# A two-layer decoder on one core: pass B of the first self attention in nine sets, statistics by chunk, and mixes in halves

## The chip, the cores and the metric

The kernel runs on one core of a Trainium2 chip. The metric is the device time of one launch in microseconds (us), and lower is better. The core has a matrix engine (TensorE, in the profile PE, with its weight loads as PEld), a vector engine (VectorE, DVE), a scalar engine (ScalarE, ACT), a general engine (GpSimd, POOL) and a synchronisation engine (SyncE, SP), which here only issues transfers. Each engine runs its own list of instructions in order; they wait for each other by semaphores.

## The reference, cut to what matters

The input x is (batch 4, sequence 1024, width 256), the context (4, 154, 256). Two decoder layers follow each other; every sublayer is added to its input and normalised.

```python
def _layernorm(x, axis=-1, eps=1e-05):
    m = mean(x); v = var(x)
    return (x - m) / sqrt(v + eps)

# layer 0: self attention, 16 heads of 16, causal
scores = einsum('bhqd,bhkd->bhqk', q * scale, k) + causal_bias
out = softmax(scores) @ v;  out = out @ w_out.T + b_out
x = layernorm(x + out)
# layer 0: cross attention, 16 heads of 64, over the 154 context rows
# layer 0: feed forward with rounded activations and weights and a convolution
# layer 1: self attention, one head of 256, softmax over axis 1
# layer 1: cross attention, 16 heads of 16, keys and values from the context, padding mask
# layer 1: feed forward
x_prev = concatenate([zeros, x[:, :-1]], axis=1)
xr = mu_r * x + (1 - mu_r) * x_prev
xk = mu_k * x + (1 - mu_k) * x_prev
out = sigmoid(xr @ W_r) * (square(relu(xk @ W_k)) @ W_v)
x = layernorm(x + out)
```

## The kernel before

All of x stays in on-chip memory for the whole launch: one tile per batch, eight chunks of 128 rows, 256 wide. Each stage function makes a list of events, `at(when, function, arguments)`, and `run_in_order` calls them by their number `when`. Every TensorE instruction and some others are marked to keep that order on their engine; the rest is placed by the framework's planner, which orders the instructions of VectorE, ScalarE and GpSimd itself. `layernorm` takes the statistics of its chunks at once (L136 and L137), asks GpSimd for the inverse root (L141), and leaves the normalising instructions (`last_step`: L156 on VectorE, or L147 and L152 on ScalarE) on a list of pending work; `run_in_order` counts six events down and then runs it, and `settle` runs all that is pending for a batch, which a function that reads x calls first.

**First self attention** (function `self_attention`, profile lines L178 to L480). Sixteen head sets of four heads follow each other, four per batch; T = 20 units of event time are one head set. For head set s two passes run at once. Pass A computes the scores with queries as rows, only to find each query's maximum (`a_unit`, L319 and L335 on VectorE). Then `shifted_queries` turns the maxima (nmt, L344 on VectorE, transposes L351 on TensorE) and adds them to the padded queries (L355), so that in pass B the scores come out less their maximum. Pass B (`b_unit`) computes the scores of head set s - 1 with keys as rows, ScalarE takes the exponential (L385), GpSimd clears the upper triangle (L388), and `weighted` multiplies by the values into an accumulator (tiles acc). Keys come in chunks of 128, queries in halves of 512; the causal triangle makes some pieces narrower: a set is what shares a bank of 512. Pass B has ten sets, the sets 2 and 9 being 256 wide, and pass A has nine units; each is done as two pairs of heads, and `together` interleaves one pair of A with one pair of B, so that the four row groups of the array hold four 32-row matmuls at once. Eighteen such pairs fill the units 1 to 18; the tenth set of B has a place of its own at 19. Then comes the boundary: the weighting of set 7 at 18.5, the tenth set at 19, the weighting of set 8 at 20.1, the shifted queries at 20.3, the weighting of set 9 at 20.4.

Seven banks of the accumulation memory hold the score tiles and everything else that TensorE makes in this stage; a new tile waits until the one seven before it was read.

Beside this stand fillers: projections of keys, queries and values, transposes, and for a finished batch the output: `normalised`, `turned_back`, and `out_projected` (tile s from wo and onT, then y = s + bias at L474 and two additions to x at L479 and L480, whose maximum and minimum with 0 leave out what is not a number). The output runs in four places per batch at 11.5 and 15.5 of two head sets, two chunks a place, with a layernorm of four chunks after every second. For the last batch they stand one after another at the end, before cross attention, whose first step is to transpose x (L652, copy xT at L655).

**Last stage** (`cross_attention_and_feed_forward`, L1215 on). Cross attention of layer 1 goes head set by head set; the exponentials are L1349, the weighted sum is acc, `normalised` is L1380 to L1384, `turned` L1396, `out_projected` L1412. For a batch that is through with it, `shifted_x` transposes x into fx with a zero column ahead (L1433, copies L1436), `mix` makes the two mixes m1 and m0 (L1442 on ScalarE, then L1443 on VectorE) from 1024 columns at a time, `squared` (L1453, L1454) and `fed_forward` (L1466 to L1469) finish, and the result is normalised on ScalarE and stored. The last batch has the same schedule as the others and nothing beside it.

The other three stages (cross attention of layer 0, feed forward and self attention of layer 1) use the same `layernorm`, after the last of four chunks was added.

## Time and profile before

| what | value |
|---|---|
| time, median of 3 runs | 2303.15 us (2297.65 to 2305.23) |
| the profiled execution | 2305.49 us |
| its span | 2303.8 us |
| first self attention | about 31 to 780 us |
| cross attention, first feed forward | about 780 to 1430 |
| self attention of layer 1, rest of the feed forward | to about 1845 |
| cross attention of layer 1, feed forward | about 1845 to 2304 |

The profile is one execution. A line of a timeline has the start in us from the span's beginning, the duration, the engine, the line of the kernel, the operation, the tiles (written <- read) with their shapes, and the count of instructions that it merges; in square brackets it says how long the engine had been idle before it and what ended that. The row PEclk of the page shows in forty slices what clock TensorE was granted, in tenths of full speed.

### The profile page before, as it was taken

How to read it: one execution, taken by the hardware profiler on the slowest of the kernel's cores; microseconds unless marked ns; L12 is line 12 of the kernel's file. 1: busy time of each engine (PE TensorE's matmuls, PEld its weight loads, DVE VectorE, ACT ScalarE, POOL GpSimd, SP SyncE). 2: the span in 40 equal slices, each digit the busy share in tenths (PEclk: the TensorE clock that was granted, in tenths of full speed). 3: DMA queues.
4: the chain of work that ended last, by engine and by line, in shares of the span. 5: the costliest groups of instructions: out<-in, count | busy, mean ns of one | idle time of the engine just before them, and what ended most of it. 6: DMA issues, size and time to landing. Idle time of an engine off the chain costs nothing.

```text
span 2303.8 us, 38032 instructions
## 1 busy us (share of the span) xinstructions
PE 2172.9 (94%) x14228; PEld 1275.8 (55%) x14228; DVE 1482.0 (64%) x3223; ACT 1127.3 (49%) x2909; POOL 507.7 (22%) x1113
## 2 busy tenths in 40 slices
PE   7999999999999999999999998879989999999996
PEld 4444444454444556656556556556666755565645
DVE  4666666666666555558997887775873365555644
ACT  1455554554455465456656664444442234434354
POOL 1111111111112265444454432000000021111101
PEclk9999999999999999999999999989999999999998
DMA  3201100000000100000000000000000010010101
GB/s 89 55 7 33 39 23 15 10 15 15 6 15 1 38 1 19 1 1 1 1 1 1 33 1 21 1 1 1 1 1 1 2 20 15 10 32 11 28 1 37
DMA packets 24440, 34.78 MB, mean 15 GB/s; under 512 B 5952, under 2 KB 19648, under 8 KB 24256
## 3 DMA queue, kind: packets, MB, share of 16 engines
q1 hardware_dynamic: 22640, 31.20, 5.8%
q8 instruction: 113, 1.85, 0.3%
q10 hardware_dynamic: 1616, 1.16, 0.2%
q14 instruction: 71, 0.58, 0.1%
HBM read 15.56 MB, written 4.19 MB: 9 GB/s over the span
## 4 chain that ended last, share of the span: by engine, by line
PE 73%; DVE 19%; ACT 5%; issue 1%; POOL 1%; DMA 1%; SPq 0%; ACTq 0%; DVEq 0%; POOLq 0%
PE s L178 22%; PE t L568 15%; PE s L1166 10%; PE s L568 9%; PE acc L178 6%; DVE gt L917 4%; PE acc L1166 3%; PE t L752 2%; ACT u L727 2%; DVE bnst L136 1%; DVE x L156 1%; DVE nmp L319 1%; DVE nmx L723 1%; PE t L1075 1%; DVE ht L903 1%
## 5 line engine op out<-in xcount | busy, mean ns | idle before, releaser
L385 ACT ACTIVATE p<-s 128x512 f32<-128x512 f32 (+1 forms) x640 | 319.5, 554 | 296.3 <-PE s L178 293.6
L319 DVE TENSOR_REDUCE nmp<-s 128x1 f32<-128x512 f32 (+3 forms) x640 | 298.9, 524 | 156.4 <-PE s L178 156.4
L178 PE MATMUL s<-qs,kp 32*128 32x512 f32 (+3 forms) x1536 | 370.1, 531 | 2.7 <-DVE nmp L319 2.7
L178 PE MATMUL s<-kp,qp 32*128 32x128 f32 (+3 forms) x2304 | 330.2, 408 | 5.6 <-DVE nmp L319 3.5
L735 POOL TENSOR_SCALAR p<-u,rs 128x128 f32<-128x128 f32 x512 | 214.5, 437 | 290.5 <-DVE rs L731 196.1
L178 PEld LDWEIGHTS s<-kp,qp 32*128 32x128 f32 x2304 | 168.0, 188 | 142.9 <-issue 43.1
L388 POOL TENSOR_SCALAR_AFFINE_SELECT p<-p 128x256 f32<-128x256 f32 x256 | 100.6, 408 | 650.1 <-ACT p L385 650.1
L727 ACT ACTIVATE u<-s,nmx 128x154 f32<-128x154 f32 x512 | 192.0, 388 | 31.6 <-DVE nmx L723 27.1
L178 PEld LDWEIGHTS s<-qs,kp 32*128 32x128 f32 x1536 | 143.9, 186 | 65.0 <-DVE nmp L319 28.0
L141 POOL TENSOR_TENSOR rstd<-ve,neghalf 128x4 f32<-128x4 f32 (+1 forms) x56 | 55.3, 987 | 539.2 <-DVE ve L139 502.1
L178 PE MATMUL acc<-p,v 128*32 128x512 f32 (+3 forms) x1536 | 164.4, 508 | 1.1 <-ACT ot L427 0.8
L568 PEld LDWEIGHTS s<-kt,qt 64*128 64x128 f32 x1024 | 102.5, 188 | 71.6 <-issue 53.6
L568 PE MATMUL s<-kt,qt 64*128 64x154 f32 x1024 | 136.5, 316 | 0.5 <-ACT qt L709 0.3
L723 DVE TENSOR_REDUCE nmx<-s 128x4 f32<-128x616 f32 x128 | 101.2, 790 | 50.2 <-PE s L568 50.2
L568 PE MATMUL t<-xT,xw 128*128 128x512 f32 x256 | 122.4, 601 | 7.5 <-DVE xT L655 4.4
L1323 DVE TENSOR_REDUCE nmt<-s 128x3 f32<-128x462 f32 (+1 forms) x192 | 99.0, 579 | 46.4 <-PE s L1166 46.4
L917 DVE SCALAR_TENSOR_TENSOR gt<-ht,cw,gt 128x256 f32<-128x256 f32 x256 | 117.9, 501 | 6.6 <-ACT gt L913 5.5
L568 PE MATMUL t<-v,pt 128*128 128x256 f32 x512 | 117.7, 383 | 3.3 <-DVE pt L1076 2.9
L568 PE MATMUL s<-qt,xT 128*128 128x512 f32 x256 | 120.0, 613 | 0.0
L568 PE MATMUL t<-xw,ot 128*128 128x256 f32 x512 | 116.3, 381 | 3.6 <-ACT pr L756 1.9
L335 DVE TENSOR_REDUCE nmp<-s 128x4 f32<-128x512 f32 x128 | 82.6, 688 | 49.9 <-PE s L178 49.9
L568 PEld LDWEIGHTS t<-v,pt 128*128 128x128 f32 x512 | 97.1, 192 | 24.3 <-issue 6.2
(257 smaller groups left out, 3886.5 us busy)
## 6 DMA issues: line engine op xcount, KB each, us to landing
qp<-sq SPq DMA_DIRECT2D x128, 64.0 KB, 2.3
kp<-sk SPq DMA_DIRECT2D x64, 64.0 KB, 2.3
out_dram<-x SPq DMA_DIRECT2D x8, 512.0 KB, 2.9
x<-in_x_dram SPq DMA_DIRECT2D x3, 1024.0 KB, 5.4
wf<-in_L_ffn_w_dram SPq DMA_DIRECT2D x2, 1024.0 KB, 5.9
xw<-in_L_xattn_wk_dram SPq DMA_DIRECT2D x1, 1024.0 KB, 5.0
xw<-in_L_xattn_wq_dram SPq DMA_DIRECT2D x1, 1024.0 KB, 5.1
xw<-in_L_xattn_wv_dram SPq DMA_DIRECT2D x1, 1024.0 KB, 5.0
```

Of the source, the lines that this page charges most:

```text
L178: pe(nc.tensor.matmul(o, l, r, start=start, stop=stop))
L319: nc.vector.tensor_reduce(nmp[:, 2 * pair + g, qc, i : i + 1], t[g][:, c0 : c0 + n], AX.X, ALU.max)
L335: nc.vector.tensor_reduce(nmp[:, 2 * pair + g, q0 : q0 + 4, 0], t[g].rearrange("p (j n) -> p j n", j=4), AX.X, ALU.max,)
L385: nc.scalar.activation(p[:, g, :total], t[g][:, :total], AF.Exp)
L388: nc.gpsimd.affine_select(out=v, in_=v, compare_op=ALU.is_ge, fill=0.0, base=0, pattern=[[0, 2], [1, P]], channel_multiplier=-1,)
L568: pe(nc.tensor.matmul(o, l, r, start=start, stop=stop))
L723: nc.vector.tensor_reduce(nmx.rearrange("p i g -> p g i"), t, AX.X, ALU.max, negate=True)
L727: nc.scalar.activation(u[:, 2 * i + g, :], t[:, g, i, :], AF.Exp, bias=nmx[:, i, g : g + 1], accum_out=ssum[:, i, g : g + 1],)
L735: nc.gpsimd.tensor_scalar(p[:, h * P : (h + 1) * P], u[:, h, :P], rs[:, h : h + 1], 1.0, ALU.mult, ALU.mult)
L917: nc.vector.scalar_tensor_tensor(g, ht[:, i, k : k + N], cw[:, hc, k : k + 1], g, ALU.mult, ALU.add)
L1166: pe(nc.tensor.matmul(o, l, r, start=start, stop=stop))
L1323: nc.vector.tensor_reduce(nmts[s % 2][:, 3 * u : 3 * u + n, g, 17], ts[g][:, : n * LK].rearrange("p (c k) -> p c k", k=LK), AX.X, ALU.max, ...
```

## The change

Pass B: the sets are now lists of (half, key chunk, place in the bank). The 256 columns of key chunk 6 go into set 2 beside the 256 of key chunk 2, so there are nine sets of 512 and no place at 19. The weighting of chunk 6 has an event of its own at 10.6, and the weighting of set 8 is the last of the head set, at 20.4, behind the shifted queries. Output: eight places with one chunk each, y in a tile of its own, and after each chunk its statistics are taken (`measured`), so `layernorm` of four chunks finds them made; the same in cross attention, in self attention of layer 1 and in both places of the last stage. Mixes: by halves of 512 columns; for batches 0 to 2 `shifted_x` stands at the same event times as before (u is 16 earlier), the mix m1 at 18.4 to 25.6 and m0 at 30.4 to 42.4. For the last batch the whole chain from the turning to the feed forward runs by halves of the sequence, and `settle` can be asked for a half. The last layernorm of all waits one event instead of six.

```diff
...
-    def settle(b=None):
-
-        for p in [p for p in pending if b in (None, p[1])]:
+    def settle(b=None, c0=None):
+
+        for p in [p for p in pending if b in (None, p[1]) and c0 in (None, p[3])]:
             pending.remove(p)
...
-    def layernorm(b, c0, n, scalar=False, then=None):
+    measures = {}
+
+    def measured(b, c):
+
+        if c % 4 == 0:
+            measures[b, c // 4] = small.tile([P, 4, nc.vector.BN_AGGR_DIM], F32, tag="bnmv", name="bnmv", bufs=6)
+        st = small.tile([P, nc.vector.BN_STATS_DIM], F32, tag="bnst", name="bnst", bufs=2)
+        nc.vector.bn_stats(st, xs[b][:, c, :])
+        nc.vector.bn_aggr(measures[b, c // 4][:, c % 4, :], st)
+
+    def layernorm(b, c0, n, scalar=False, then=None, wait=6):
...
         xb = xs[b][:, c0 : c0 + n, :]
-        st = small.tile([P, 4, nc.vector.BN_STATS_DIM], F32, tag="bnst", name="bnst", bufs=2)
-        mv = small.tile([P, 4, nc.vector.BN_AGGR_DIM], F32, tag="bnmv", name="bnmv", bufs=3)
-        for c in range(n):
-            nc.vector.bn_stats(st[:, c, :], xb[:, c, :])
-            nc.vector.bn_aggr(mv[:, c, :], st[:, c, :])
+        if n == 4:
+            mv = measures.pop((b, c0 // 4))
+        else:
+            st = small.tile([P, 2, nc.vector.BN_STATS_DIM], F32, tag="bnst2", name="bnst2", bufs=2)
+            mv = small.tile([P, 2, nc.vector.BN_AGGR_DIM], F32, tag="bnmv2", name="bnmv2", bufs=3)
+            for c in range(n):
+                nc.vector.bn_stats(st[:, c, :], xb[:, c, :])
+                nc.vector.bn_aggr(mv[:, c, :], st[:, c, :])
         ve = small.tile([P, 4], F32, tag="ve", name="ve", bufs=2)
...
         rstd = small.tile([P, 4], F32, tag="rstd", name="rstd", bufs=3)
...
-        pending.append([6, b, last_step])
+        pending.append([wait, b, last_step, c0])
...
-        b_sets = [(0, [(0, 0)]), (0, [(1, 0), (3, 384)]), (0, [(2, 0)])]
-        b_sets += [(1, [(k, 0)]) for k in range(4)]
-        b_sets += [(1, [(4, 0)]), (1, [(5, 0), (7, 384)]), (1, [(6, 0)])]
+        b_sets = [[(0, 0, 0)], [(0, 1, 0), (0, 3, 384)], [(0, 2, 0), (1, 6, 256)]]
+        b_sets += [[(1, k, 0)] for k in range(5)]
+        b_sets += [[(1, 5, 0), (1, 7, 384)]]
...
         def b_unit(s, i, pair):
-            qh, pieces = b_sets[i]
+            pieces = b_sets[i]
             t = [bank() for _ in range(2)]
...
             rows = [slice(64 * pair + 32 * g, 64 * pair + 32 * g + 32) for g in range(2)]
-            total = sum(width(qh, kc) for kc, _ in pieces)
             rounds = []
-            for kc, c0 in pieces:
+            for qh, kc, c0 in pieces:
                 n = width(qh, kc)
...
                     (
...
                 for g in range(2):
-                    nc.scalar.activation(p[:, g, :total], t[g][:, :total], AF.Exp)
-                for c0 in [c0 for kc, c0 in pieces if kc >= 4 * qh]:
+                    nc.scalar.activation(p[:, g, :], t[g], AF.Exp)
+                for c0 in [c0 for qh, kc, c0 in pieces if kc >= 4 * qh]:
                     v = p[:, :, c0 : c0 + P]
...
                         out=v, in_=v, compare_op=ALU.is_ge, fill=0.0, base=0,
...
-        def weighted(s, i):
+        def weighted(s, qh, i, pieces, first=False, last=False):
             b, t4 = divmod(s, 4)
-            qh, pieces = b_sets[i]
-            first, last = i in (0, 3), i in (2, 9)
             if first:
...
             acc = accs[s, qh]
-            p2 = [pts.pop((s, i, pair)) for pair in range(2)]
+            p2 = [pts[s, i, pair] for pair in range(2)]
             for kc, c0 in pieces:
...
                 for g in range(4):
...
                         first,
-                        last,
+                        last and kc == pieces[-1][0],
                     )
...
                 if qh == 0:
...
-        def out_projected(b, i):
+        def out_projected(b, c):
             onT = ots[b, "n"]
-            t = bank()
-            for j in range(2):
-                c = 2 * i + j
-                for e in range(2):
-                    mm(
-                        t[:, j * E : (j + 1) * E],
-                        onT[:, e, c * P : (c + 1) * P],
-                        l0a_wo[:, e, :],
-                        e == 0,
-                        e == 1,
-                    )
-            y = wk.tile([P, 2, 512], F32, tag="p", name="y0", bufs=6)[:, :, :E]
-            nc.vector.tensor_tensor(
-                y, t.rearrange("p (c n) -> p c n", c=2), bo2.unsqueeze(1).to_broadcast([P, 2, E]), ALU.add
-            )
-
-            xb = xs[b][:, 2 * i : 2 * i + 2, :]
+            t = bank()[:, :E]
+            for e in range(2):
+                mm(t, onT[:, e, c * P : (c + 1) * P], l0a_wo[:, e, :], e == 0, e == 1)
+            y = wk.tile([P, E], F32, tag="y0", name="y0")
+            nc.vector.tensor_tensor(y, t, bo2, ALU.add)
+
+            xb = xs[b][:, c, :]
             nc.vector.scalar_tensor_tensor(xb, y, 0.0, xb, ALU.max, ALU.add)
             nc.vector.scalar_tensor_tensor(xb, y, 0.0, xb, ALU.min, ALU.add)
-            if i % 2:
-                layernorm(b, 2 * i - 2, 4)
+            measured(b, c)
+            if c % 4 == 3:
+                layernorm(b, c - 3, 4)
...
                 at(t0 + 5 * T + 3.5 + 4 * i, turned_back, b, e, q)
-                at(t0 + (i // 2 + 7) * T + (11.5, 15.5)[i % 2] if b < 3 else t0 + 6 * T + i, out_projected, b, i)
+            for c in range(NC):
+                u = (117.5, 135.5, 151.5, 155.5, 157.5, 171.5, 175.5, 177.5)[c]
+                at(t0 + u if b < 3 else t0 + 6 * T + c, out_projected, b, c)
         for i in range(2 * NB):
...
             for q in range(2):
...
                 at((s + 2) * T + 1.5 + 4 * i, normalised, s, i)
-            for i in range(10):
-                at((s + 1) * T + (2 * i + 4.5 if i < 8 else 20.1 + 0.3 * (i - 8)), weighted, s, i)
+            t0 = (s + 1) * T
+            at(t0 + 4.5, weighted, s, 0, 0, [(0, 0)], True)
+            at(t0 + 6.5, weighted, s, 0, 1, [(1, 0), (3, 384)])
+            at(t0 + 8.5, weighted, s, 0, 2, [(2, 0)], False, True)
+            for k in range(5):
+                at(t0 + 10.5 + 2 * k, weighted, s, 1, 3 + k, [(k, 0)], k == 0)
+            at(t0 + 10.6, weighted, s, 1, 2, [(6, 256)])
+            at(t0 + 20.4, weighted, s, 1, 8, [(5, 0), (7, 384)], False, True)
         for i, (w, name) in enumerate(((l0x_wk, "k"), (l0x_wq, "q"), (l0x_wv, "v"))):
...
         for s in range(4 * NB + 1):
...
                 at(s * T + 1 + j, together, *units)
-            if s > 0:
-                at(s * T + 19, together, *[(b_unit, s - 1, 9, pair) for pair in range(2)])
         run_in_order(events)
...
             nc.vector.tensor_tensor(xs[b][:, c, :], t[:, :E], xs[b][:, c, :], ALU.add)
+            measured(b, c)
             if k == 3:
...
             )
+            measured(b, c)
             if c % 4 == 3:
...
             nc.vector.tensor_tensor(xb, t.rearrange("p (c n) -> p c n", c=2), xb, ALU.add)
+            for c in range(2 * i, 2 * i + 2):
+                measured(b, c)
             if i % 2:
...
         def shifted_x(b, e, q):
-            settle(b)
+            settle(b, 4 * q)
             t = bank()
...
                 pe(nc.tensor.transpose(
...
-        def mix(b, i, e):
-            if e == 0:
+        def mix(b, i, e, q):
+            if (e, q) == (0, 0):
                 mixed[b, i] = wk.tile([P, 2, S], F32, tag=f"m{i}", name=f"m{i}", bufs=1)
-            m = mixed[b, i][:, e, :]
-            nc.scalar.activation(m, fx[:, e, 0:S], AF.Copy, scale=omu[:, e, i : i + 1])
-            nc.vector.scalar_tensor_tensor(m, fx[:, e, 1:], mus[:, e, i : i + 1], m, ALU.mult, ALU.add)
+            m = mixed[b, i][:, e, q * 512 : (q + 1) * 512]
+            nc.scalar.activation(m, fx[:, e, q * 512 : (q + 1) * 512], AF.Copy, scale=omu[:, e, i : i + 1])
+            nc.vector.scalar_tensor_tensor(
+                m, fx[:, e, 1 + q * 512 : 1 + (q + 1) * 512], mus[:, e, i : i + 1], m, ALU.mult, ALU.add
+            )
...
             if (m, q) == (0, 0):
...
                 c0 = 2 * k - 2
+                for c in range(c0, c0 + 4):
+                    measured(b, c)
                 stored = out[b].rearrange("(c p) d -> p c d", p=P)[:, c0 : c0 + 4, :]
                 layernorm(
-                    b, c0, 4, True, lambda: nc.sync.dma_start(out=stored, in_=xs[b][:, c0 : c0 + 4, :])
+                    b, c0, 4, True, wait=6 if b < NB - 1 else 1, then=lambda: nc.sync.dma_start(out=stored, in_=xs[b][:, c0 : c0 + 4, :])
                 )
...
                 at(t0 - 16.7 + 0.6 * i, x_transposed, b, e, q)
-                at(t0 + 5 * T + 9.1 + 0.6 * i, turned, b, e, q)
-                at(t0 + 5 * T + 12.3 + 1.7 * i, out_projected, b, i)
-            u = t0 + 6 * T + 5
-            for i in range(4):
-                e, q = divmod(i, 2)
-                at(u + 0.6 * i, shifted_x, b, e, q)
-                at(u + 10.3 + 6 * i, squared, b, e, q)
-                at(u + 37.2 + 8 * i, fed_forward, b, i)
-            for e in range(2):
-                at(u + 2.6 + 0.1 * e, mix, b, 1, e)
-                at(u + 2.8 + 0.1 * e, mix, b, 0, e)
+            u = t0 + 5 * T + 9
+            if b < NB - 1:
+                for i in range(4):
+                    e, q = divmod(i, 2)
+                    at(u + 0.1 + 0.6 * i, turned, b, e, q)
+                    at(u + 3.3 + 1.7 * i, out_projected, b, i)
+                    at(u + 16 + 0.6 * i, shifted_x, b, e, q)
+
+                    at(u + 18.4 + 2.4 * i, mix, b, 1, i % 2, i // 2)
+                    at(u + 26.3 + 6 * i, squared, b, i % 2, i // 2)
+                    at(u + 30.4 + 4 * i, mix, b, 0, i % 2, i // 2)
+                    at(u + 53.2 + 8 * i, fed_forward, b, i)
+            else:
+
+                for q in range(2):
+                    for e in range(2):
+                        at(u + 1 + 6 * q + e, turned, b, e, q)
+                        at(u + 4 + 6 * q + e, out_projected, b, 2 * q + e)
+                        at(u + 20 + 3 * q + e, shifted_x, b, e, q)
+                        at(u + 22 + 5.5 * q + 0.1 * e, mix, b, 1, e, q)
+                        at(u + 25 + 5 * q + e, squared, b, e, q)
+                        at(u + 27 + 6 * q + 0.1 * e, mix, b, 0, e, q)
+                        at(u + 28 + 6 * q + e, fed_forward, b, 2 * q + e)
         for s in range(4 * NB):
...
             if s % 2 == 0:
...
                 at(t0 + 13 + 7 * q, weighted, s, q)
-                at(t0 + T + 3 + q, normalised, s, q)
+                at(t0 + T + 3 + q if s < 4 * NB - 1 else t0 + T + (3, 12.5)[q], normalised, s, q)
         run_in_order(events)
...
```

## The prediction

> **What bounds the kernel now.** I read the page first (busy shares, the row of granted clock, the chain that ended last), then the timelines of TensorE and VectorE at the places that the change touches, then a table of stretches for the clock.
>
> ```profile
> PE 2172.9 (94%) x14228; PEld 1275.8 (55%) x14228; DVE 1482.0 (64%) x3223; ACT 1127.3 (49%) x2909; POOL 507.7 (22%) x1113
> PEclk9999999999999999999999999989999999999998
> PE 73%; DVE 19%; ACT 5%; issue 1%; POOL 1%; DMA 1%; SPq 0%; ACTq 0%; DVEq 0%; POOLq 0%
> ```
>
> TensorE is busy 94% of the span and is 73% of the chain, so time is won only by taking work off TensorE, by closing one of its stalls, or by avoiding half clock after a stall. The stalls are where to look. Timeline of a quiet head-set boundary of the first stage (TensorE, then VectorE):
>
> ```profile
> 102.80 1.07 PE L178 MATMUL acc<-p,v 128*32 128x512 f32 x8
> 103.80 0.71 PE L178 MATMUL s<-qs,kp 32*128 32x256 f32 x8
> 104.44 1.14 PE L178 MATMUL acc<-p,v 128*32 128x384 f32 x16
> 105.51 1.09 PE L351 MATMUL s<-ident,nmt 128*128 128x128 f32 x8
> 106.53 0.64 PE L178 MATMUL acc<-p,v 128*32 128x256 f32 x8
> ...
> 104.23 0.26 DVE L344 TENSOR_REDUCE nmt<-nmp 128x32 f32<-128x96 f32 x1
> ```
>
> Differences of starts, with set 8's at 104.44 and set 9's at 106.53: 1.00 + 0.64 + 1.07 + 1.02 + 0.57 = 4.30 us. The tenth set (103.80) and the weighting at 104.44 cover nmt, which is ready at 104.49: no stall. The same boundary where a layernorm of four chunks falls:
>
> ```profile
> 412.41 0.69 DVE L474 TENSOR_TENSOR y<-s,bo 128x512 f32<-128x512 f32 x1 [0.50 <-PE s L178]
> 413.13 0.69 DVE L479 SCALAR_TENSOR_TENSOR x<-y,x 128x512 f32<-128x512 f32 x1
> 413.86 0.69 DVE L480 SCALAR_TENSOR_TENSOR x<-y,x 128x512 f32<-128x512 f32 x1
> 414.59 0.75 DVE L136 BATCH_NORM_STATS2 bnst<-x 128x6 f32<-128x256 f32 x2
> ...
> 416.32 0.48 PE L178 MATMUL s<-kp,qp 32*128 32x128 f32 x2 [0.66 <-DVE nmp L319]
> ```
>
> VectorE works three microseconds on the output, the row maxima come late, and TensorE waits for a bank. That stands at five boundaries, and at three of them half clock follows:
>
> ```profile
> 549.00:556.00 7.00, 6.16 (x48) 3.24 (x48) 5.84 (x19) 3.06 (x6) 2.14 (x4) 0.80 0.00 1
> 729.00:736.00 7.00, 6.16 (x48) 2.52 (x40) 6.58 (x21) 3.11 (x6) 2.85 (x6) 0.87 0.00 0
> 1973.00:1980.00 7.00, 3.77 (x26) 1.61 (x20) 6.64 (x9) 5.32 (x8) 0.00 (x0) 0.76 0.00 0
> ```
>
> (Columns: length, then busy time and instructions of PE, PEld, DVE, ACT, POOL, then the granted clock.) The third row is the last stage, where four mixes stand ahead of the exponentials that free TensorE's banks; it repeats at 2082.61 and 2191.64.
>
> ```profile
> 1972.01 4.45 ACT L1442 ACTIVATE m<-fx,omu 128x1024 f32<-128x1024 f32 x4
> 1976.37 2.03 ACT L1349 ACTIVATE p<-s 128x512 f32<-128x512 f32 x4
> 1977.00 1.39 PE L1166 MATMUL s<-kt,qp 32*128 32x154 f32 x10 [3.22 <-ACT p L1349]
> ...
> 787.08 0.66 DVE L655 COPY xT<-t 128x512 f32<-128x512 f32 x1
> 787.80 2.87 PE L568 MATMUL t<-xT,xw 128*128 128x512 f32 x4 [3.66 <-DVE xT L655]
> ```
>
> The last two lines are the hand-over to cross attention, a stall of 3.66 us behind a VectorE copy.
>
> **The change, part by part** (us; plus is slower).
>
> *Pass B in nine sets.* TensorE streams the same columns; 40 exponentials per head set become 36. The boundary loses the tenth set (0.64) and the last weighting place (0.57), in all 1.21, but these were nmt's cover: TensorE now goes from the weighting of set 7 straight to the transposes of nmt. nmt is ready 1.69 after that weighting starts, it lasts 1.00, so the stall is 0.7: boundary 1.00 + 0.7 + 1.02 + 1.07 = 3.8, or -0.5. The 256 columns come back in set 2: its pair of units grows from 3.13 (with four transposes) to the 3.55 that a full pair with four transposes takes, +0.4, and their weighting, moved behind set 3, adds 0.43 (a 16-matmul weighting less an 8-matmul one, 1.0 to 1.43). Together +0.25 per head set, 15 sets, less 0.5 in the sixteenth: +3.5. Without the 0.7 stall it would be -7; with 1.5 of it, +15.
>
> *Output in eight places.* A pair of units with an output place takes 4.07 against 2.96 without: +1.1, four per batch. A place is now four matmuls (0.86 at 0.215 each) for eight (1.72, of which 0.6 went into the pair's own wait for a bank), so 0.26 if the same 0.6 is hidden and 0.86 if nothing is; four transposes, the nearest filler, cost 3.55 - 2.96. I take +0.6 each, eight per batch: 4.8 against 4.4, +1 over three batches. What it removes is the VectorE block. The five boundaries cost, last pair to the end of set 8's weighting, 4.41 and 1.42 for 3.04 and 1.07 (1.72, twice in batch 0), 10.2 for 5.75 (4.45, twice in batch 1), 8.60 for 5.75 (2.85, batch 2): 15.2. Against it: per chunk VectorE runs y 0.42, two updates 0.42 each, statistics 0.42 and 0.17, about 1.8 in all, and three places per batch stand at 17.5, right ahead of the last pair's maxima and nmt. A projection at 17.5 (two copies of 0.69) made nmt 0.11 later and the next weighting 1.25 for 1.07; I take +0.6 for each of nine, 0 and +1.5 as ends: +5.4. At the third of these in a batch the normalisation of four chunks (4 x 0.44) can stand there too.
>
> [...] Adding up for each 3.41 us window the streaming time of every matmul (0.83 ns per f32 column, times its share of the array: 32 of 128 rows is a quarter) gives 0.33 for the window before 553.2, 0.25 before 734.1, 0.40 at 365.5, where nothing followed; over the span every window at 0.36 or less is followed by half clock, none at 0.39 or more. The ordinary window here has 0.73. A stall of 0.7 in it leaves 0.73 x 2.7/3.4 = 0.58: safe. One of 1.7 leaves 0.37: on the edge, if one window holds it all. So I put new half clock only at the three fullest boundaries, chance about one half, 1.7 to 3.4 each: +3. [...]
>
> First stage: 3.5 + 1 - 15.2 + 5.4 + 3 = -2.3.
>
> *Hand-over to cross attention.* The last batch's output comes in eight chunks, so VectorE runs 24 operations of 0.42 for 12 of 0.69 (+1.8), and in the changed instruction order the normalisations of eight chunks (1.68 + 1.38), two small scalings and kt stand before the xT copy that the 3.66 stall waits for; before they stood behind it. xT comes 3.5 to 4 later; half clock follows already. +4 (2 to 6). Next late is the first qt.
>
> *Statistics by chunk elsewhere.* Same instructions, same durations (0.42 and 0.17), spread. A block of four (two rows of 0.75 and 0.30: 2.1) leaves the front of maxima in cross attention, where TensorE stalls of 0.5 to 1.1 stand. I take -1.5; where VectorE is some 75% busy (1358 to 1650) a shifted order can cost too: -6 to +4.
>
> *Mixes in halves, three batches.* ScalarE's order becomes two half mixes, the two fx copies, a half mix, first exponential, half mix, two exponentials, half mix, fourth exponential. The halved row would be 4.45/8 = 0.56. [...] The single idle of 3.22 becomes 0.6 and 1.5, but with thin matmuls between, so that a window can still fall under 0.36: I give 0.7 to it. Before, 6.83, 6.83 and 3.41 at half clock cost 8.5; I keep 5 of that. [...]
>
> *Tail.* Output, turning and mixes of the last batch go by halves. But VectorE's order still puts the first half's normalisation behind the second half's statistics, and all 16 transposes stand ahead of the first squared product, so that starts at 2269 to 2270 as now. The last normalisation no longer waits for its partner: four ACTIVATEs at the end for eight in 4.04, less what was hidden: -1.5 (-4 to +2).
>
> Sum: -2.3 + 4 - 1.5 - 6.8 - 1.5 = -8.1. The profiled execution took 2305.5 (span 2303.8), 2.3 over the median of 2303.15, so this is 2297 on the profile and about **2295** as a median.
>
> **Rivals.** *Half clock at the boundaries (slower).* nmt's cover is gone at every head set. If the waits are longer than I read (1.7 rather than 0.7, since maxima of four tiles queue before nmt), windows fall under 0.36 and each stretch costs 1.7 to 3.4 beside the longer stall of 1.0. That is about 3.5 per boundary; it overtakes the forecast gain of 8 from the third and is slower beyond 0.3% from the fifth of 15. With seven, 24 - 8 = +16: 2319. For it: the stretch at 549. Against it: 0.58 worked out above. *All of the clock comes back.* No new half clock (-3), the three late stretches vanish (-5), 17.5 places cost nothing (-5): 2282. For it: VectorE idles between the maxima. *Nothing net.* A hand-over of 6 (+2), 17.5 places at 1.2 (+5.4) and a tail of 0 (+1.5) eat what the layernorm blocks give: 2304. *It doesn't do what it says* only in part: the tail's halves are the likeliest to be without effect, and that is in the sum.
>
> **How the numbers follow.** Forecast 2295, own range 2288 to 2301: 0.45. Clock returns, 2282: 0.18. Nothing net, 2304: 0.15. Half clock at boundaries, 2319: 0.22. A measurement here can tell about 0.3%, 6.9 us: faster is below 2296.2, slower above 2310. Faster: 0.18 + 0.29 of the first = 0.47; slower: 0.22 + 0.03 from the nothing-net case = 0.25; same 0.28. The range reaches 2281 to 2315: below it and above it 0.1 each.
>
> **What would show it.** The order acc, idle of 0.7, transposes of nmt at each boundary (right), or 1.5 and more with a clock below 1 (the slower rival); no half clock at 553, 604, 734; the xT copy some 4 us after its transposes' old distance; exponentials between half mixes at 1974 and whether the clock stays 1.0; four ACTIVATEs before the last store. The forecast is wrong if the 17.5 places stall more than 1.5, or the planner's new order costs VectorE time in the middle stages, which the sum leaves at near nothing.

## The result

The changed kernel takes 2320.9 us (median of 15 runs, 2303.4 to 2325.9) against 2303.16 (15 runs, 2297.4 to 2313.2): ratio 1.0066, 95% interval 1.0051 to 1.008. It is slower by some 15 us, where 8 less was forecast. The profiled execution took 2324.1 us, span 2322.4, so the traces differ by 18.6.

From the page of the changed kernel (busy shares, granted clock, chain that ended last by engine):

```profile
PE 2164.3 (93%) x14196; PEld 1282.9 (55%) x14228; DVE 1495.2 (64%) x3287; ACT 1123.2 (48%) x2861; POOL 505.3 (22%) x1113
PEclk9999999999999999999999999989999999999998
PE 71%; DVE 19%; ACT 6%; issue 2%; POOL 1%; DMA 1%; SPq 0%; ACTq 0%; POOLq 0%; DVEq 0%
```

TensorE's work did not grow; its idle time did, from 130.9 us to 158.1, and its time at half clock, from 132.6 to 142.5. Four landmarks of each trace say where (us; the first transpose of cross attention, the first and last matmul of acc<-pr,vr, the end):

| stretch | before | changed | difference | forecast |
|---|---|---|---|---|
| first self attention | 783.0 | 799.5 | +16.5 | -2.3 |
| the three middle stages, with the hand-over | 1095.3 | 1101.2 | +5.9 | +2.5 |
| last stage, with three batches' mixes | 366.9 | 358.8 | -8.1 | -6.8 |
| tail | 58.5 | 62.8 | +4.3 | -1.5 |

Most of it lies in the first stage. Two rows of a table of stretches from 60 to 780 us, the kernel before first (columns as in the prediction; behind the clock stand the transfers' share of their engines and GB/s): TensorE is idle for 11.7 us before and for 33.8 now.

```profile
60.00:780.00 720.00, 708.34 (x6047) 347.07 (x6047) 459.14 (x978) 369.41 (x726) 106.42 (x262) 0.98 0.09 19
60.00:780.00 720.00, 686.22 (x5927) 345.39 (x5958) 454.19 (x985) 358.14 (x654) 102.79 (x257) 0.98 0.08 18
```

A quiet boundary, TensorE then VectorE, in the timeline of the changed kernel:

```profile
101.76 1.06 PE L191 MATMUL acc<-p,v 128*32 128x512 f32 x8
103.59 1.06 PE L364 MATMUL s<-ident,nmt 128*128 128x128 f32 x8 [0.76 <-DVE nmt L357]
104.59 1.07 PE L191 MATMUL acc<-p,v 128*32 128x384 f32 x16
...
103.19 0.26 DVE L357 TENSOR_REDUCE nmt<-nmp 128x32 f32<-128x96 f32 x1
```

That is the forecast to the tenth: 1.83 + 1.00 + 1.00 = 3.83, with a wait of 0.76. Set 2's pair is 3.56 (3.55 forecast). And here is the second of the three boundaries of batch 0 that have an output place at 17.5, where a normalisation falls too (same two timelines):

```profile
371.93 0.41 DVE L476 TENSOR_TENSOR y<-s,bo 128x256 f32<-128x256 f32 x1
372.38 0.43 DVE L479 SCALAR_TENSOR_TENSOR x<-y,x 128x256 f32<-128x256 f32 x1
372.84 0.43 DVE L480 SCALAR_TENSOR_TENSOR x<-y,x 128x256 f32<-128x256 f32 x1
373.30 0.43 DVE L136 BATCH_NORM_STATS2 bnst<-x 128x6 f32<-128x256 f32 x1
373.76 0.18 DVE L137 BATCH_NORM_AGGREGATE bnmv<-bnst 128x2 f32<-128x6 f32 x1
373.86 1.38 DVE L332 TENSOR_REDUCE nmp<-s 128x1 f32<-128x128 f32 x4
375.17 1.37 DVE L169 TENSOR_SCALAR x<-x,bnmv,rstd 128x256 f32<-128x256 f32 x4
376.45 0.25 DVE L357 TENSOR_REDUCE nmt<-nmp 128x32 f32<-128x96 f32 x1
...
372.47 1.06 PE L191 MATMUL acc<-p,v 128*32 128x512 f32 x8
376.76 1.18 PE L364 MATMUL s<-ident,nmt 128*128 128x128 f32 x8 [3.22 <-DVE nmt L357]
377.87 1.51 PE L191 MATMUL acc<-p,v 128*32 128x384 f32 x8
```

Read the starts on VectorE: the output block holds it from 371.93 to 373.86, so the last four maxima, which in the quiet boundary start as the weighting starts, start 1.39 after it; the normalisation takes another 1.28. Nothing of TensorE's lies over the sum. Such waits stand at eight of the fifteen boundaries: 2.01 (three times), 3.22 (three), 2.27 (two), against 0.69 to 0.79 at the other seven. Half clock follows seven of the eight:

```profile
280.00:287.00 7.00, 4.88 (x45) 3.27 (x47) 3.23 (x9) 0.96 (x3) 0.76 (x2) 0.76 0.22 36
375.50:382.50 7.00, 5.58 (x52) 3.74 (x53) 3.13 (x9) 1.49 (x3) 0.00 (x0) 0.76 0.22 37
423.50:430.50 7.00, 4.64 (x48) 3.17 (x46) 3.57 (x10) 0.85 (x3) 1.74 (x3) 0.76 0.11 19
748.00:755.00 7.00, 6.40 (x36) 3.16 (x40) 2.16 (x7) 1.67 (x3) 0.14 (x1) 0.62 0.00 1
1994.00:2001.00 7.00, 6.41 (x32) 3.45 (x32) 6.62 (x13) 6.18 (x12) 0.00 (x0) 0.61 0.00 1
2102.00:2109.00 7.00, 6.93 (x41) 2.37 (x39) 6.61 (x13) 5.81 (x11) 0.00 (x0) 1.00 0.00 0
```

(A table of stretches, columns as before.) Seven stretches from 282 to 750 us, 27.3 us in all. The last two rows are the mixes of the first batch, where 6.83 us at half clock stay, and of the second, where the clock is now whole, as it is in the third's. From the changed kernel's timeline, three lines of the first batch's mixes, with half mixes between the exponentials, then the hand-over and the tail:

```profile
1997.44 1.06 ACT L1358 ACTIVATE p<-s 128x512 f32<-128x512 f32 x2
1998.39 0.72 ACT L1453 ACTIVATE m<-fx,omu 128x512 f32<-128x512 f32 x1
1999.00 0.59 ACT L1358 ACTIVATE p<-s 128x512 f32<-128x512 f32 x1
...
806.48 0.67 DVE L662 COPY xT<-t 128x512 f32<-128x512 f32 x1
807.21 3.78 PE L575 MATMUL t<-xT,xw 128*128 128x512 f32 x4 [6.61 <-DVE xT L662]
2303.44 2.93 PE L1175 MATMUL s<-wv,ka 128*128 128x256 f32 x6 [2.79 <-ACT ka L1467]
```

At the hand-over the wait grew from 3.66 to 6.61, about as forecast. The wait of 2.79 us in the tail was not foreseen.

### The profile page after: what moved, and what is told of

It reads as the page before. It is cut to its first block, busy times and chain, and to the rows that moved or that the text cites. A ratio compares the mean times of both kernels' runs of the same rounds, so it can differ in the third digit from the quotient of the medians.

```text
span 2322.4 us, 37976 instructions
## 1 busy us (share of the span) xinstructions
PE 2164.3 (93%) x14196; PEld 1282.9 (55%) x14228; DVE 1495.2 (64%) x3287; ACT 1123.2 (48%) x2861; POOL 505.3 (22%) x1113
## 4 chain that ended last, share of the span: by engine, by line
PE 71%; DVE 19%; ACT 6%; issue 2%; POOL 1%; DMA 1%; SPq 0%; ACTq 0%; POOLq 0%; DVEq 0%
PE s L191 21%; PE t L575 15%; PE s L1175 10%; PE s L575 9%; PE acc L191 6%; DVE gt L925 3%; PE acc L1175 3%; DVE nmp L332 2%; PE t L759 2%; ACT u L734 2%; DVE x L169 1%; DVE nmx L730 1%; PE t L1083 1%; DVE bnst L136 1%; PE s L364 1%
## 5 line engine op out<-in xcount | busy, mean ns | idle before, releaser
L397 ACT ACTIVATE p<-s 128x512 f32<-128x512 f32 x576 | 312.8, 596 | 281.2 <-PE s L191 266.5
L400 POOL TENSOR_SCALAR_AFFINE_SELECT p<-p 128x256 f32<-128x256 f32 x256 | 99.7, 407 | 660.5 <-ACT p L397 660.5
L191 PEld LDWEIGHTS s<-qs,kp 32*128 32x128 f32 x1536 | 151.4, 186 | 43.8 <-DVE nmp L332 19.3
L575 PE MATMUL t<-xT,xw 128*128 128x512 f32 x256 | 123.3, 604 | 10.2 <-DVE xT L662 6.6
```

Source lines behind the costliest of these rows:

```text
L191: pe(nc.tensor.matmul(o, l, r, start=start, stop=stop))
L397: nc.scalar.activation(p[:, g, :], t[g], AF.Exp)
L400: nc.gpsimd.affine_select(out=v, in_=v, compare_op=ALU.is_ge, fill=0.0, base=0, pattern=[[0, 2], [1, P]], channel_multiplier=-1,)
L575: pe(nc.tensor.matmul(o, l, r, start=start, stop=stop))
```

## The experiments

All are ratios to the kernel before, measured in the same rounds; they are not the quotients of the medians that the text names. The runs were made on four chips: 1 to 4 on one, 5 to 8 on a second, 9 to 12 and 16 to 18 on a third, 13 to 15 on a fourth. They are numbered in the order in which they were made. "Old last batch" means the last batch on the schedule of the others, its last normalisation after six events.

| run | pass B sets | output places | last batch | ratio (95%) |
|---|---|---|---|---|
| changed kernel | 9 | 8, three at 17.5 | changed | 1.0066 (1.0051 to 1.008) |
| 13, the same again | 9 | 8, three at 17.5 | changed | 1.0058 (1.0031 to 1.0084) |
| 1 | 9 | 8, none at 17.5 | changed | 1.0009 (0.9987 to 1.0031) |
| 7 | 9, set 8's weighting ahead of nmt | 8, three at 17.5 | changed | 1.0046 (1.0031 to 1.0061) |
| 3 and 14 | 9 | 8, three at 17.5 | old | 1.0065 (1.0041 to 1.0089), 1.0051 (1.0031 to 1.0071) |
| 6 | 10 | 8, three at 17.5 | changed | 0.9972 (0.9959 to 0.9984) |
| 9 | 10 | 8, three at 17.5 | old | 0.9932 (0.991 to 0.9954) |
| 10 | 10 | 8, none at 17.5 | old | 0.9942 (0.9923 to 0.9961) |
| 2 and 18 | 10 | 4 | changed | 0.9972 (0.9951 to 0.9993), 0.9958 (0.9937 to 0.998) |
| 12 | 10 | 4 | changed, one wait later | 0.9937 (0.9911 to 0.9962) |
| 8 and 17 | 10 | 4 | old | 0.9927 (0.9912 to 0.9941), 0.9929 (0.9903 to 0.9954) |
| 11, statistics spread in the first stage too | 10 | 4 | old | 0.9923 (0.9903 to 0.9942) |
| 15 | 9, set 8's weighting ahead of nmt | 8, none at 17.5 | old | 0.9952 (0.9934 to 0.997) |
| 16 | the same | 8, none at 17.5 | changed | 0.9984 (0.9963 to 1.0006) |
| 4, mixes alone | 10 | 4 | old, whole statistics | 0.9955 (0.994 to 0.9969) |
| 5, nine sets alone | 9 | 4 | old, whole mixes | 1.005 (1.003 to 1.007) |

**The places at 17.5 (run 1).**

```diff
-                u = (117.5, 135.5, 151.5, 155.5, 157.5, 171.5, 175.5, 177.5)[c]
+                u = (121.6, 135.5, 151.5, 155.5, 161.6, 171.5, 175.5, 181.6 if b < 2 else 177.5)[c]
```

> The changed kernel with the three output places of each batch that stood at 17.5 moved behind the boundary, to 1.6 of the next head set (the third one of batch 2, where no nmt follows, stays). Theory A (the output's VectorE block of 2.06 us stands ahead of the last pair's maxima and makes nmt late): the waits of 2.07, 3.28 and 2.34 us before the transposes of nmt fall to the 0.8 of the quiet boundaries, 14 us in eight places less, and the seven half-clock stretches between 280 and 750 us go with them, about 10 us more, so 2296 to 2303 against 2319. Rival B (nine sets took the cover away everywhere, the places hardly matter): within 4 us of the changed kernel, 2314 to 2322.

2306.66 us, 13 below the changed kernel's first measurement by the ratios. That is the direction of theory A and not rival B, but short of the 16 to 23 that A gave. In the traces the waits before the transposes of nmt fall by 12.0 of the 14 us, and the first stage by 14.0 of the 24. The boundary that had 2.01 now has, in run 1's timeline,

```profile
280.14 1.06 PE L191 MATMUL acc<-p,v 128*32 128x512 f32 x8
281.90 1.06 PE L364 MATMUL s<-ident,nmt 128*128 128x128 f32 x8 [0.69 <-DVE nmt L357]
282.89 1.07 PE L191 MATMUL acc<-p,v 128*32 128x384 f32 x16
```

Two waits of 2.05 stay, where the normalisation of four chunks still stands ahead of nmt, and after each a stretch of 3.41 us at half clock; the other five stretches between 282 and 750 are gone.

**First stage and mixes by themselves (runs 2 and 4).** Run 2 puts `b_sets`, `b_unit`, `weighted`, the place at 19 and four output places back as they were, with the statistics taken in one block. Run 4 is the kernel before with the new `mix` and its event times:

```diff
-            for e in range(2):
-                at(u + 2.6 + 0.1 * e, mix, b, 1, e)
-                at(u + 2.8 + 0.1 * e, mix, b, 0, e)
+            for i in range(4):
+                at(u + 2.4 + 2.4 * i, mix, b, 1, i % 2, i // 2)
+                at(u + 14.4 + 4 * i, mix, b, 0, i % 2, i // 2)
-                at(u + 10.3 + 6 * i, squared, b, e, q)
+                at(u + 10.3 + 6 * i, squared, b, i % 2, i // 2)
```

> The changed kernel with pass B and the output places of the first self attention as before (ten sets, four places), everything else changed. If the loss lies in that stage and the hand-over: the last stage's 8 us remain, the tail's cost remains (+4), so 2297 to 2302, a little below the kernel before. If the loss lies in the statistics by chunk or the tail: 2308 or more.

> The kernel before with the mixes in halves alone, at the event times of the change, for all four batches. As the prediction's term: 6.8 us less than before, 2296; the trace of the changed kernel gives 8.0 for three batches, 2295. Rival (the exponentials only move, the half-clock stretches stay): 3 less, 2300.

2299.95 and 2292.93 us. The first stage carries the loss; everything else together is a gain, yet a smaller one than the mixes alone, 10.4 us by the ratio. Run 4 has half mixes in all four batches: in its trace the stretch of three batches is 8.0 us shorter than before and the tail 3.9. So something outside the first stage costs in run 2.

**The last batch (runs 3, 12, 14, 16 to 18).**

```diff
-            if b < NB - 1:
+            if b < NB:
-                    b, c0, 4, True, wait=6 if b < NB - 1 else 1, then=...
+                    b, c0, 4, True, then=...
-                at(t0 + T + 3 + q if s < 4 * NB - 1 else t0 + T + (3, 12.5)[q], normalised, s, q)
+                at(t0 + T + 3 + q, normalised, s, q)
```

> The changed kernel with the last batch on the schedule of the other three batches (mixes in halves, but one half after the other not followed through to the output, last normalisation after six events). The trace shows the last 70 us 4.3 us longer than before. If the halves of the last batch cause it: 3 to 6 us less than the changed kernel. If it was only where half clock fell in that execution: within 2 us of it.

> The third run again, beside the changed kernel: the last batch on the schedule of the others. If the last batch's halves cost in the changed kernel what they cost with ten sets (9 us between the sixth and the ninth run): 2306 to 2312. If the third run was right: within 3 us of the changed kernel.

> The changed kernel itself once more, on the chip and in the rounds of the next two runs, so that they can be set against it directly: 2315 to 2321 by its first measurement.

In two pairs, the changed kernel against run 3 and run 13 against run 14, the ratios show no difference (13 against 14: 1.0058 and 1.0051). With ten sets the medians differ:

> The eighth run again (ten sets, four places, mixes in halves, statistics by chunk outside the first stage, old last batch), as the fastest so far, beside the next: 2284 to 2290.

> The second run again: the seventeenth with the changed schedule of the last batch. If the halves of the last batch cost 8 us here: 2293 to 2298, and 7 to 10 above the seventeenth. If the first comparison only met different chips: within 3 of it.

2285.29 and 2291.92 us, 6.6 apart; and with nine sets but free boundaries

> The fifteenth run with the changed schedule of the last batch. Nothing is left of the blocked boundaries, so the last batch's halves stand alone: if they cost 7 to 9 us whatever stands before, 2299 to 2301 where the fifteenth run has 2291 to 2292; if they cost nothing with nine sets, within 3 us of it.

2299.1 where run 15 has 2291.42. The intervals of the last two pairs overlap; those of 2 and 8 and of 6 and 9 don't, but these were made on two chips. All four go the same way, by 6.6 to 10 us. The traces are clearer: from the last acc<-pr,vr to the end it is 55.9 us with the old last batch (runs 3, 8 to 11, 14, 15 and 17), and 62.8 in the changed kernel and in runs 2, 6, 7, 13 and 16; runs 1 and 18 have 59.7.

So the traces of runs 3 and 14 have the 7 us too. The single executions suggest what hides them in the medians. In run 13 seven of twelve had a granted clock of 0.976 to 0.980 and took 2304.3 to 2311.3 us, five had 0.967 to 0.969 and took 2323.2 to 2328.2. In run 14 only four were of the first sort (0.975 to 0.979, 2302.7 to 2310.3), the others (0.969 to 0.971) took 2313.4 to 2319.2. Among executions of like clock run 14 is the shorter, by about 9 us at the lower clock and about 2 at the higher. Why only 2 there stays open.

What the halves cost can be seen on ScalarE in the changed kernel's timeline:

```profile
2299.83 2.07 ACT L165 ACTIVATE x<-x,nmr,rstd 128x256 f32<-128x256 f32 x4 [1.76 <-DVE nmr L160]
2301.81 0.57 ACT L1466 ACTIVATE ka<-s 128x512 f32<-128x512 f32 x1
2302.29 0.58 ACT L1479 ACTIVATE th<-s 128x512 f32<-128x512 f32 x1
2302.77 0.62 ACT L1467 ACTIVATE ka<-ka 128x512 f32<-128x512 f32 x1
```

The first half's normalisation, which waits only one event, goes ahead of the second half's relu and square; TensorE waits 2.79 for ka and then runs at half clock for 6.83. Run 12 changes only that wait:

```diff
-                    b, c0, 4, True, wait=6 if b < NB - 1 else 1, then=...
+                    b, c0, 4, True, wait=1 if b == NB - 1 and k == 3 else 6, then=...
```

> The second run with the first half's last normalisation of the last batch waiting six events again, so that its four ACTIVATEs no longer stand between the half's relu and square on ScalarE. If that block is what the last batch's halves cost (a wait of 2.8 us for ka and half clock after it in the traces of the changed kernel and the second and sixth runs), 4 to 7 us below the second run, 2293 to 2296. If the cost is elsewhere (transposes and half clock at the layernorm of the halves): within 2 us of it.

2293.38 us, 0.35% below run 2 and 0.21 below its repeat, run 18; both intervals overlap. In its trace the wait for ka is gone,

```profile
2278.99 1.89 PE L1183 MATMUL s<-fw,m 128*128 128x256 f32 x8
2280.72 1.89 PE L1183 MATMUL s<-wv,ka 128*128 128x256 f32 x8
```

and from the last acc<-pr,vr to the end it is 57.5 us for run 2's 62.8: most of the 7 us were this one wait and the half clock behind it.

**Nine sets alone, ten sets back, and cover (runs 5 to 7).** Run 5 brings only the nine sets into the kernel before, run 6 takes only them out of the changed one. Run 7 is

```diff
-            at(t0 + 20.4, weighted, s, 1, 8, [(5, 0), (7, 384)], False, True)
+            at(t0 + 20.2, weighted, s, 1, 8, [(5, 0), (7, 384)], False, True)
```

> The kernel before with pass B in nine sets alone (output in four places, one layernorm block, whole mixes). The trace of the changed kernel gives +0.3 us for each quiet head set (boundary 3.8 for 4.3, set 2 +0.43, weighting +0.43), about +4. At the five layernorm boundaries nmt was ready 2.9 us after the weighting of set 7 with 1.64 of cover beside that weighting; now there is none, so 1.2 to 1.9 more each and more windows at half clock. Theory A' (the two parts need each other's room: cover and VectorE time ahead of nmt): 2308 to 2318. Rival (nine sets cost only what quiet sets show): 2306 to 2309.

> The changed kernel with pass B in ten sets again, its tenth set and set 8's weighting back ahead of nmt, output in eight places with the three at 17.5. Theory A': the cover of about 1.7 us comes off waits of 2.07, 3.28 and 2.34, leaving 0.4, 1.6 and 0.7; fewer windows fall to half clock; 15 to 20 us less than the changed kernel, 2297 to 2305. Rival (the block at 17.5 costs the same whatever the cover): 4 us less, 2313 to 2317.

> The changed kernel with one event moved: the weighting of set 8 ahead of the shifted queries (20.2 for 20.4), so that 1.0 us of TensorE's work lies over the wait for nmt. Quiet boundaries lose up to 0.8 of wait, less what the weighting then waits for its exponentials (0 to 0.6); the eight blocked ones lose 1.0 and some half clock: 10 to 18 us less than the changed kernel, 2301 to 2309. Rival (the weighting waits for its exponentials as long as it covered): within 4 of it.

Run 5: 2313.92 us, +11.5 by the ratio, of which quiet sets explain 4. Run 6: 2298.33, 22 us below the changed kernel. So nine sets cost about twice as much beside the output places as alone (0.94% and 0.5%), while eight places cost nothing with ten sets (run 6 against runs 2 and 18). The two changes need the same room. Run 6's timeline at the boundary that waited 2.01:

```profile
276.59 1.06 PE L191 MATMUL acc<-p,v 128*32 128x512 f32 x8
277.59 0.71 PE L191 MATMUL s<-qs,kp 32*128 32x256 f32 x6
278.77 0.69 PE L191 MATMUL s<-qs,kp 32*128 32x256 f32 x2 [0.48 <-DVE nmp L332]
279.40 1.07 PE L191 MATMUL acc<-p,v 128*32 128x384 f32 x16
280.40 1.09 PE L364 MATMUL s<-ident,nmt 128*128 128x128 f32 x8
```

VectorE's block is there as before (nmt starts at 279.41), but the tenth set and a weighting lie over it. The clock stays whole: from 66.7 to 780 us run 6 has no half clock at all (the same table of stretches, whose first 6.7 us are still at half clock),

```profile
60.00:780.00 720.00, 701.47 (x6042) 348.19 (x6072) 470.81 (x1039) 370.58 (x726) 109.13 (x265) 1.00 0.09 20
```

Run 7 gains 4.6 us by the ratio, less than half of what was expected, and the intervals overlap. In its trace a quiet boundary has

```profile
98.61 2.72 PE L191 MATMUL acc<-p,v 128*32 128x512 f32 x24
101.26 1.09 PE L364 MATMUL s<-ident,nmt 128*128 128x128 f32 x8
```

The start of the transposes is 2.65 behind that of the first weighting. The changed kernel had 1.83 there, with set 8's weighting (1.00) still to come, so only some 0.2 is won: set 8's weighting waits for its own tiles, which GpSimd clears last (L400 after the exponential L397). From its table of waits over 60 to 780 us (who waited for whom, us, times, longest):

```profile
PEld acc L191 <- POOL p L400: 28.8, 56, 2.2
```

The changed kernel has 7.8 there. So the rival had its part: the waits before nmt fall from 29.3 us to 8.7, but at a quiet boundary the cover only moved the wait, and the first four quiet head sets are 0.3 to 0.8 longer than the changed kernel's. What this trace gains is the half clock: none follows a boundary, and the first stage is 783.2 us, 16.3 less than the changed kernel's (3.2 of it ahead of the first boundary). The median of all executions shows less of that, and why stays open.

**The statistics and the places (runs 8 to 11, and 15).** Run 8 is run 2 with the old last batch, run 9 is run 6 with it, run 10 has run 1's places as well; run 11 calls `measured` for each pair of chunks in the first stage; run 15 puts runs 1, 3 and 7 together.

> The kernel before with the mixes in halves (all batches on one schedule) and the statistics by chunk outside the first stage; in the first stage the statistics are still one block. It differs from the second run by the last batch's schedule, from the fourth by the statistics. If statistics by chunk cost nothing: 2293, as the mixes alone. If they cost the 3 us that the second run's trace loses in the self attention of layer 1: 2296. If the last batch's halves are what the second run loses against the fourth, this run is 4 to 7 us below the second.

> Ten sets in pass B, output in eight places (three at 17.5), statistics by chunk everywhere, mixes in halves, the last batch on the schedule of the others. Beside the eighth run it tells eight places from four when nmt has its cover: no half clock from 60 to 780 us in the trace of the sixth run, where the eighth has one stretch, but waits of 0.2 to 1.4 at eight boundaries and a hand-over 3.7 later. Theory: 0 to 5 us slower than the eighth run, 2286 to 2291, and 8 to 12 faster than the sixth. Rival (eight places gain by themselves): below 2283.

> The ninth run with the three places at 17.5 moved to 1.6 of the next head set. The waits left at the boundaries with cover go (1.2 + 0.8 + 1.4 us in each batch, 8 us in all by the sixth run's trace); behind the boundary the places can take 0.6 to 1.0 each. Theory: 2 to 6 us below the ninth run. Rival (the ninth run's cover is enough, the places only move): within 2 us.

> The eighth run with the statistics taken with each output place of two chunks in the first stage too, instead of four chunks at the end: 1.05 us of the layernorm block leave the boundary. The five boundaries of 4.41 or more come down by up to 1 us each and the one stretch at half clock may go: 2 to 6 us below the eighth run, 2280 to 2284. Rival (planner moved the statistics already; waits come from the output's own 2 us): same as the eighth.

> Nine sets with everything that the runs showed to help: no place at 17.5, set 8's weighting over the wait for nmt, the last batch on the old schedule. If nine sets lose only through what stands between the last maxima and nmt, this is near the runs with ten sets: 2290 to 2296. If they lose beside that by their own 0.3 a head set and by set 8's weighting waiting for its exponentials (2.65 for two weightings where 2.0 is the work): 2298 to 2304.

Run 8, 2285.61 us, beats both kernels, and its repeat (2285.29) says the same. It is 0.28% below run 4. That would be some 6 us for the statistics by chunk outside the first stage, where the forecast had 1.5. It is not shown: the intervals just meet at 0.994 (run 17's overlaps run 4's), the runs were made on different chips, and the middle stages, where most of the change lies, are as long in the traces (1090.9 us in run 4, 1092.1 in run 8, 1088.9 in run 17). Between the first and the last acc<-pr,vr run 8's trace has no half clock, run 4's has 6.8 us. Runs 9, 10 and 11 can't be told from run 8: eight places neither gain nor cost when nmt has its cover, and off 17.5 or on it is then the same, against the expectation of 2 to 6. Run 15 comes to 2291.42: nine sets lose little by themselves, as run 15's forecast for that case had it.

## Why the prediction was wrong

*The sum of the first stage* failed: -2.3 forecast, +16.5 in the trace.

- The step "A projection at 17.5 (two copies of 0.69) made nmt 0.11 later ... I take +0.6 for each of nine" took the wrong yardstick. The projection's work is not on VectorE; in the trace of the kernel before it is

```profile
145.42 0.69 ACT L276 ACTIVATE sk<-s,bk 128x512 f32<-128x512 f32 x1 [0.70 <-PE s L178]
```

  so its 0.11 said nothing of a VectorE block. The nearest row was the layernorm boundary shown ahead of it, where VectorE's block did delay the maxima. The block at 17.5 starts just after the first of the last pair's two groups of maxima, 0.7 us before the weighting, and takes 2.06: +1.25 to +2.45 at eight boundaries beyond the quiet wait, 3 x 1.26 + 3 x 2.47 + 2 x 1.52 = 14.2 for 5.4. Run 1 takes 12.0 of them away with the places; the rest are the two waits of 2.05 where the normalisation stands alone, which the step named ("can stand there too") and left without a cost.
- "New half clock ... +3" followed from it. The sums over windows fit the changed trace too (0.351 or less before half clock, 0.375 or more elsewhere), but were applied to waits of 0.7 to 1.7 instead of 2.0 to 3.2. Seven stretches, 27.3 us, cost up to half of that, 13.6, an estimate from the distance of matmuls in the changed trace (256 columns of f32 over the whole array: 0.427 us at half clock, 0.216 at full). (The head set from the transposes at 425.85 us to those at 473.29, with a wait 1.32 longer and 3.41 us at half clock, takes 2.96 more than in run 1, so about 1.6 for the stretch.) With 14.2 + 13.6 in place of 5.4 + 3 the sum is +17.1; measured +16.5. That they meet so nearly is in part luck: up to the first transposes of nmt the changed trace is 2.2 us ahead, and behind the last ones it takes 6.2 more, of which half clock explains up to 3.4.
- Quiet boundary and set 2 were as worked out. The step's own sum was not: -0.5 + 0.4 + 0.43 is +0.33 for each head set and not +0.25, and 15 x 0.25 - 0.5 is 3.25 and not 3.5; the first four quiet head sets are 0.21 to 0.34 longer, so little hangs on it. The places and the five layernorm blocks were not measured by themselves. The half clock at 553, 604 and 734 is gone, as forecast, and seven stretches stand for three.

The rival "half clock at the boundaries" had the mechanism, the place and the end (2319); it was given a chance of 0.22. It spoke of maxima queueing before nmt, but did not name the output block as what they queue behind.

*Hand-over*: right in place and size; the wait for xT grew by 2.95 us, and the lag of the changed trace behind the trace before grew from 16.45 at the first transpose to the 19.65 at which it stays, 3.2 for 4. *Mixes*: right, -8.1 for -6.8 in the traces, -10.4 by run 4 with the fourth batch's halves in it. Of the -6.8, 3.5 was the clock (8.5 less 5); the other 3.3, for exponentials that come earlier, was the author's estimate, and no run shows that term. The changed trace shows in its place a half mix of 0.72 alone and 0.61 from start to start in a row, and 3.32 from fx to the first exponential (1992.48 to 1995.80), where the trace before has 6.3 (1970.1 to 1976.37); half clock stands at the first batch's mixes alone, for 6.83, where there were 6.83, 6.83 and 3.41. *Statistics elsewhere*: open. The trace has the middle stages +2.7 beside the hand-over, with 6.8 us more at half clock, where -1.5 was forecast; the medians of runs 4, 8 and 17 say some 6 less. *Tail*: wrong sign. The step "less what was hidden: -1.5" looked at the four ACTIVATEs at the end and not at where the first four go: they stand ahead of ka. It cost 7 us in the traces, 6.6 to 10 in the medians of four pairs, and in those of two others nothing that could be told from the way single executions fell.

The ratios, run to run: mixes -0.45%, statistics by chunk -0.27 (mean of runs 8 and 17), last batch +0.4 (mean of runs 2 and 18, less that mean: 0.37), eight places with cover +0.07 (run 6 less the mean of 2 and 18), nine sets on top of that +0.94. The sum is +0.66, the changed kernel's ratio; the chain of runs makes it so, and the single terms are uncertain by about 0.2 each.

## What to carry to other kernels

Before taking work off TensorE at a place where it waits for nothing, ask what that work was lying over, and price the wait from VectorE's own list of instructions there, by engine: a filler whose epilogue runs on ScalarE says nothing of one on VectorE. Two changes that are cheap alone can use the same slack: measure one without the other. And look at the clock behind a wait: here a wait of 2.01 us and a stretch of 3.41 us at half clock are some 3.6 us together, an estimate from the 1.6 worked out above for the stretch.

## What the runs showed of the hardware

These are our own counts from the clock records and the matmuls of this case's traces, where nothing else is said those of the kernel before and the changed one. That they hold for other kernels is not shown.

- Both records have only two values, full clock and half of it. Matmuls of 256 columns of f32 over the whole array start 0.216 us apart at full clock and, in the changed trace, 0.427 at half clock; those of 512 columns 0.429 and 0.853.
- The stretches at half clock last 3.41, 6.83 or 10.24 us, save those at the two kernels' ends (8.35 and 7.98). In each trace their starts lie whole multiples of 3.413 us apart, to within 0.01 (553.24 and 604.44 in the kernel before are fifteen apart). Counted from the span's beginning, the first of these marks is at 0.28 us in the trace before and at 2.16 in the changed one.
- Cut at these marks into windows and summed as in the prediction (streaming time times the share of the array, bf16 at half the time of f32), the windows at full clock from 15 us on are 631 in the trace before, and half clock follows 24: all of 0.357 or less and none of 0.393 or more. In the changed trace they are 634, and half clock follows 27: all of 0.351 or less and none of 0.375 or more.
- The longest idle time of TensorE in a window tells them apart less well: the best line for both traces, 1.75 us, puts 16 of the 1265 windows on the wrong side. Half clock followed the window at 549.8 us of the trace before, whose longest idle time is 0.66 (sum 0.33), and not the one at 2290.6, which has 1.89 (sum 0.39).
- Of the eight long waits before the transposes of nmt in the changed trace, half clock followed those of 3.22 us (three) and of 2.01 (three) and one of the two of 2.27. The other one, from 614.83 to 617.10, lies in two windows; the first, at 613.1, has a sum of 0.382.
- In all twenty traces together there are some 12,690 windows at full clock from 15 us on, and half clock follows 416. A line at a sum of 0.36 puts 20 of them on the wrong side, all between 0.26 and 0.40; the best line by the longest idle time, 1.8 us, puts 172. The edge is not sharp: in run 1 a window of 0.378 was followed by half clock, and those of 0.366 and 0.329 were not.

The same first stage had 34.1 us at half clock up to the first transpose in the trace of the kernel before and 10.2 in run 4's, and ended 10.8 us apart without any change there. In run 1 four executions with a granted clock of 0.981 took 2289.2 to 2292.3 us, and ten with 0.971 to 0.973 took 2303.7 to 2309.2. Single executions of one kernel lie up to 25 us apart (run 2), and the profiled one is only one of them.
